# Preparing the second layer's weights half a period after the first layer's, in a two-layer attention kernel on one core

## The chip, the cores and the metric

The kernel runs on one core of a Trainium2 chip. The metric is the device time of one execution in microseconds. Before the change the median of three runs is 3221.76 us (3221.34 to 3221.77).

## What is computed

The input is x of shape [16, 512, 128]. Two blocks follow one another, each of the form x + s * silu(f):

```python
xn = layernorm(x)
s  = gated_conv(xn)          # projection, two causal depthwise convolutions of 32 taps, gates, projection
g  = silu(local_ffn(xn))     # DEPTH = 2 layers, see below
x  = x + s * g
xn = layernorm(x)
s  = attention16(xn)         # 16 heads of 8 with rope
g  = silu(soft_moe(xn))      # 8 experts of 64 slots
x  = x + s * g
```

The part that the change touches is the two-layer function. Each of its layers does

```python
q, k, v = split(shift_token(x) @ wqkv)          # 8 heads of 64
q = rotary(l2norm(q) * qs); k = rotary(l2norm(k) * ks)
x = x + local_attention(q, k, v, window=64) @ wo
h = layernorm(shift_token(x)) * lg + lb
a, gate = split(h @ w1 + b1)                    # 2 x 341 columns
x = x + (a * gelu(gate)) @ w2 + b2
```

## The kernel before

**Streams.** The 16 batches run through stages that are Python generators: L0 (first layer, `layer(b, 0)`), L0b (second layer, `layer(b, 1)`), A (the sum of the first block and the projections of the second, `pre`), S1 and S2 (the attention with 16 heads), M (the experts, `moe`). Two more generators run once: C, the convolution of all batches (`conv`, lines 741 to 853), and P, the preparation of the weights (`setup`, lines 225 to 279).

**Order.** Lines 935 to 954 merge the generators with a heap. PLAN gives each stage a start and a length in periods, a period being the time of one batch; each `yield` returns a weight, and the next piece of a generator is due at its last due time plus weight / total * length. Pieces are written out in the order in which they are due. That order is the priority with which a scheduler then places the instructions on the queues of the engines (TensorE or PE, VectorE or DVE, ScalarE or ACT, GpSimd or POOL, and SP, which issues nearly all DMAs). Each queue runs in order, and an instruction that waits holds up all that stand behind it. C starts at -0.2 of a period and takes 1.8; P starts at -0.01 with a length of 0.009, so nearly the whole of it is due before the first layer's first piece at 0.0. L0b of batch 0 is due from 1.43 on.

**What P does.** It loads small tables (lg, wcol, qkb, line 227 to 234), the rotation tables rt (line 237), and fills `mean` with 1/128 (line 239). Then, for each layer l: six products of rt with the head scales make rot (lines 242 to 251); four pieces of wqkv are loaded (line 254), split into a rounded part and its remainder (lines 256 and 257) and written to the DRAM tensor wqd (line 258); wo, w1 and w2 are loaded (lines 260 to 263); b1 is corrected with six small matmuls (line 268) and sums (line 269); w1 is scaled and freed of its mean (lines 270 to 274), split (lines 276 and 277) and written to the DRAM tensor w1d (line 278).

**What L0 does.** `proj(c)`, for four pairs of heads, loads a piece of wqd on POOL's queue (line 323), multiplies (lines 221 to 223), and forms squares, rotated values and norms on ScalarE, VectorE and POOL (lines 335 to 355). `turn` transposes (lines 364 and 367), `attend` computes the attention (lines 379 to 418). Line 429 loads w1 from w1d, line 433 applies wo, lines 460 to 472 are the second half of the layer.

**What C does.** Its first part goes through the 16 batches: load x into one of two buffers xA (line 771), statistics (lines 146 to 154), scaling (line 776), store of xnd (line 777), transposes (line 780), store of xnTd (line 782), products into Z (lines 789 and 790). L0 of batch b reads xnd and xnTd. Then come the 13 steps of the Toeplitz products (lines 798 to 824) and the 24 output steps (lines 826 to 850), and all of it a second time for the other half of the channels, with the sums read from `part` (line 835) and the result written to s0d (line 844), which stage A reads. After it `late` (line 855) loads the weights of the second block.

**Buffers.** NBUF (lines 30 to 35) gives the number of buffers of each ring of tiles; a tile takes the next buffer of its ring and waits until the last reader of the old tile is done. P draws on the rings of the layers: "q" (4), "wq" (2), "rt" (2), "kT" (2), "w1" (1). The experts' ring "sb" has 2 buffers, for e (lines 679 and 724), ct (line 726) and slT (line 698). All of M's products and transposes take their PSUM bank from "a", which has one buffer and which A, S1 and S2 use as well (lines 36 and 37).

Of the kernel before, what the change touches and what calls it, by code (L numbers as in the profile page):

```python
# [10 lines left out]
F32 = mybir.dt.float32  # L11
F32R = mybir.dt.float32r
AF = mybir.ActivationFunctionType
ALU = mybir.AluOpType
# [8 lines left out]
HID = 341  # L23
CH = [(0, 128), (128, 128), (256, 85)]
# [20 lines left out]
TOT = {"C": 204.0, "P": 11.0, "L0": 93.0, "A": 24.0, "S1": 57.0, "S2": 52.6, "M": 33.0}  # L45
# [48 lines left out]
def bc_row(ap, parts):  # L94
    return ap.rearrange("(o d) -> o d", o=1).to_broadcast([parts, ap.shape[0]])


def body(ctx, tc, a):
    nc = tc.nc
    NB = a["x"].shape[0]  # L100
    V, S, G, PE = nc.vector, nc.scalar, nc.gpsimd, nc.tensor
    dma = nc.sync.dma_start
    bcp = NW * NB

    const = ctx.enter_context(tc.tile_pool(name="const", bufs=1))
# [86 lines left out]
    def mk(sid, b, dflt):  # L192
        def tl(shape, tag, dt=F32):
            cnt[0] += 1
            tg = f"{tag}{sid}"
            return pools[sid].tile(shape, dt, tag=tg, name=f"{tag}{sid}_{b}_{cnt[0]}", bufs=NBUF.get(tg, 2))

        def pt_(nm, tag=dflt):
            cnt[0] += 1
            alt = TAIL.get((tag, NB - b))  # L200
            if alt:
                turns_[tag] = turns_.get(tag, 0) + 1
                tag = alt[turns_[tag] % len(alt)]
            return psb.tile([128, 512], F32, tag=TAGS[tag], name=f"{nm}{sid}_{b}_{cnt[0]}", bufs=NPSUM[TAGS[tag]])

        def quad(src, nm, tag=dflt):
            pt = pt_(nm, tag)
            for p in range(4):
                PE.transpose(pt[:, p * 128 : p * 128 + 128], src(p), ident)  # L209
            return pt  # L210

        def split(pt, tag):
            t = tl([128, 2, 512], tag, F32R)
            S.copy(t[:, 0, :], pt)
            V.tensor_tensor(t[:, 1, :], pt, t[:, 0, :].bitcast(F32), ALU.subtract)  # L215
            return t

        return tl, pt_, quad, split

    def mm3(out, lh, ll, rh, rl, start=True, stop=True):  # L220
        PE.matmul(out, lh, rh, start=start, stop=False)  # L221
        PE.matmul(out, lh, rl, start=False, stop=False)  # L222
        PE.matmul(out, ll, rh, start=False, stop=stop)  # L223

    def setup():
        tl, pt_, quad, split = mk("0", 0, "tr0")
        lg = tl([128, 4], "lg")
        dma(out=lg, in_=a["lgb"])
        dma(out=b1.rearrange("p l k j -> p (l k j)"), in_=a["b1p"])
        wcol = tl([128, 1], "wc")  # L230
        dma(out=wcol, in_=a["wcol"])
        dma(out=maskf.rearrange("p i k -> p (i k)"), in_=a["mask"])
        qkb = tl([128, 2, 2, 64], "q")
        dma(out=qkb.rearrange("p l i d -> p (l i d)"), in_=bc_row(a["qks"], 128))
        V.tensor_scalar(qkb[:, :, 0, :], qkb[:, :, 0, :], 8.0, None, ALU.mult)
        rt = tl([128, 4, 4, 64], "rt")
        dma(out=rt.rearrange("p i n d -> p (i n d)"), in_=a["rot"])
        mean = tl([128, 128], "kT")
        G.memset(mean, 1.0 / 128.0)
        yield 1  # L240
        for l in range(2):
            for i in range(4):
                sc = qkb[:, l, i // 2, :]
                if i % 2:
                    for k in range(2):
                        V.tensor_tensor(
                            rot[:, l, 1, :, i // 2, 32 * k : 32 * k + 32], rt[:, i, :, 32 * k : 32 * k + 32],
                            sc[:, None, 32 - 32 * k : 64 - 32 * k].to_broadcast([128, 4, 32]), ALU.mult,
                        )
                else:  # L250
                    V.tensor_tensor(rot[:, l, 0, :, i // 2, :], rt[:, i], sc[:, None, :].to_broadcast([128, 4, 64]), ALU.mult)
            for c in range(4):
                w = tl([128, 384], "q")
                dma(out=w, in_=a["wqkv"][l, :, 384 * c : 384 * c + 384])
                wt = tl([128, 2, 384], "wq", F32R)
                V.tensor_copy(wt[:, 0, :], w)
                V.tensor_tensor(wt[:, 1, :], w, wt[:, 0, :].bitcast(F32), ALU.subtract)
                dma(out=wqd[l, c].bitcast(F32), in_=wt.bitcast(F32))
                yield 1
            dma(out=wo[:, l], in_=a["wo"][l].rearrange("(c p) d -> p c d", p=128))  # L260
            w1 = tl([128, 2 * HID], "rt")
            dma(out=w1, in_=a["w1"][l])
            dma(out=w2[:, l].rearrange("p j d -> p (j d)"), in_=a["w2p"][l])
            V.tensor_scalar(w2[:, l, 2, :], w2[:, l, 2, :], wcol, None, ALU.mult)
            for k in range(2):
                for j, (r, n) in enumerate(CH):
                    pb = pt_("pb")
                    PE.matmul(pb[:n, 0:1], w1[:, k * HID + r : k * HID + r + n], lg[:, 2 * l + 1 : 2 * l + 2], start=True, stop=True)
                    V.tensor_tensor(b1[:n, l, k, j : j + 1], b1[:n, l, k, j : j + 1], pb[:n, 0:1], ALU.add)
            V.tensor_scalar(w1, w1, lg[:, 2 * l : 2 * l + 1], None, ALU.mult)  # L270
            for k in range(2):
                pb = pt_("pb")
                PE.matmul(pb[:, 0:HID], mean, w1[:, k * HID : k * HID + HID], start=True, stop=True)
                V.tensor_tensor(w1[:, k * HID : k * HID + HID], w1[:, k * HID : k * HID + HID], pb[:, 0:HID], ALU.subtract)
            ws = tl([128, 2, 2 * HID], "w1", F32R)
            V.tensor_copy(ws[:, 0, :], w1)
            V.tensor_tensor(ws[:, 1, :], w1, ws[:, 0, :].bitcast(F32), ALU.subtract)
            dma(out=w1d[l].bitcast(F32), in_=ws.bitcast(F32))
            yield 1

    def load_x(tl, b, tag):
        x = tl([128, 4, 128], tag)
# [572 lines left out]
    def late():  # L855
# [83 lines left out]
        "L0": lambda b: layer(b, 0, box), "L0b": lambda b: layer(b, 1, box), "A": pre, "S1": first, "S2": second,  # L939
        "M": lambda b: moe(b, xrs, prs),  # L940
        "C": lambda b: conv(), "P": lambda b: setup(),
    }
    tot = dict(TOT, L0b=TOT["L0"])
    heap = [(b + st, k, b, nm, ln, make[nm](b)) for b in range(NB) for k, (nm, st, ln) in enumerate(PLAN)]
    heap.append((CONV0, -1, 0, "C", CONV, make["C"](0)))
    heap.append((-0.01, -2, 0, "P", 0.009, make["P"](0)))
    heapq.heapify(heap)
    acc = {}
    while heap:
        t, k, b, nm, ln, gen = heapq.heappop(heap)  # L950
        w = next(gen, None)
# [60 lines left out]
def program(arrays):  # L1012
    import concourse.bacc as bacc

    nc = bacc.Bacc("TRN2", target_bir_lowering=False, num_devices=1)
    a = {}
    named = {}
    for k, v in arrays.items():
        named[f"in_{k}_dram"] = v
        a[k] = nc.dram_tensor(f"in_{k}_dram", v.shape, mybir.dt.from_np(v.dtype), kind="ExternalInput").ap()  # L1020
    a["out"] = nc.dram_tensor("out_0_dram", arrays["x"].shape, F32, kind="ExternalOutput").ap()
    with tile.TileContext(nc, schedule_with_timeline_sim=TLS) as tc, ExitStack() as ctx:
        body(ctx, tc, a)
    return nc, named
# [8 lines left out]
```

## Time and profile before

The page is that of one profiled execution.

| what | value |
|---|---|
| median of three runs | 3221.76 us |
| profiled execution, its own time | 3220.23 us |
| span of the profile | 3218.4 us |
| mean granted clock of TensorE | 0.974 |
| busy: PE | 2932.7 us, 91% of the span |
| busy: PEld, DVE, ACT, POOL | 2173.2, 2334.5, 2071.7, 1596.0 us |
| the chain that ended last | PE 57%, DVE 17%, ACT 13%, POOL 5%, issue 4%, DMA 3% |
| DMA | 251.55 MB, mean 78 GB/s; 249 GB/s in the first of 40 slices |

The span lacks 1.83 us of the execution's own time. A slice is 80.5 us long. "PEld" is the loading of weights into TensorE, "SPq" the issuing of DMAs by SP, "granted clock" the share of full speed that TensorE ran at. A line of a timeline has the start and the length in us, the engine, the line of the kernel, the operation, the tile written and the tile read, how many instructions it stands for, and in brackets the idle time before it and what ended it. An arrow reads "written from".

### The profile page before, as it was taken

Reading aid. Unit: us, or ns where it says so; the run is one execution under the profiler, and the core shown is the slowest. Engines: PE = TensorE matmul, PEld = TensorE weight load, DVE = VectorE, ACT = ScalarE, POOL = GpSimd, SP = SyncE. Lnnn points to the kernel's source line nnn. Section 1 sums busy time; section 2 is a strip of 40 time slices with the busy share of each in tenths; the row PEclk is TensorE's granted clock in tenths of the full one; section 3 lists DMA queues with packets and bytes.
Section 4 is the critical chain, followed back from the end, with each engine's and each line's share of the span. In section 5 each row is a group of like instructions: output and inputs, shape, how many; then the busy total and the mean of one; then the engine's idle time right before and its main releaser. Section 6 shows DMA issues by size and latency. Waiting matters only on the chain.

```text
span 3218.4 us, 67550 instructions
## 1 busy us (share of the span) xinstructions
PE 2932.7 (91%) x24164; PEld 2173.2 (68%) x24164; DVE 2334.5 (73%) x7165; ACT 2071.7 (64%) x4803; POOL 1596.0 (50%) x1854
## 2 busy tenths in 40 slices
PE   5798878889999999999999999999999999999897
PEld 4687756566767767676767677676767676666553
DVE  5779567768777877777787778777777778776563
ACT  2645445657766766676666667676766766656565
POOL 2424366655546473745556464747465564542200
PEclk7999979999999999999999999999999999999998
DMA  7555443122222222222222221221222222211110
GB/s 249 146 141 131 109 118 95 51 81 65 79 65 66 64 79 73 53 82 61 79 66 84 58 76 54 78 73 53 83 59 80 67 82 57 72 51 50 29 46 18
DMA packets 199549, 251.55 MB, mean 78 GB/s; under 512 B 57488, under 2 KB 123184, under 8 KB 199216
## 3 DMA queue, kind: packets, MB, share of 16 engines
q1 hardware_dynamic: 180784, 196.90, 21.4%
q0 software_dynamic: 18432, 50.34, 6.0%
q8 instruction: 193, 3.16, 0.4%
q14 instruction: 140, 1.15, 0.1%
HBM read 159.84 MB, written 57.50 MB: 68 GB/s over the span
## 4 chain that ended last, share of the span: by engine, by line
PE 57%; DVE 17%; ACT 13%; POOL 5%; issue 4%; DMA 3%; SPq 1%; POOLq 0%; DVEq 0%; ACTq 0%
PE pvd L602 7%; PE s2d L618 5%; PE s1c L583 5%; PE pw L433 3%; DVE mw L584 3%; ACT sd L620 3%; PE pw L471 3%; PE sc L379 2%; PE pq L221 2%; PE prT L209 2%; PE ppb L714 2%; DVE pr L392 2%; ACT pr L396 2%; PE pq L223 2%; PE pq L222 2%
## 5 line engine op out<-in xcount | busy, mean ns | idle before, releaser
L584 DVE TENSOR_REDUCE mw<-s1c 128x1 f32<-128x512 f32 x1024 | 697.9, 685 | 260.3 <-PE s1c L583 253.0
L620 ACT ACTIVATE sd<-s2d 128x512 f32<-128x512 f32 x1024 | 612.4, 603 | 331.5 <-PE s2d L618 325.2
L618 PE MATMUL s2d<-QS,KS 128*128 128x512 f32 x1024 | 479.6, 471 | 44.7 <-ACT sd L620 39.7
L583 PE MATMUL s1c<-KS,QS 128*128 128x512 f32 x1024 | 454.5, 446 | 51.8 <-DVE mw L584 43.5
L354 POOL TENSOR_TENSOR y<-ss,mhalf 128x8 f32<-128x8 f32 x256 | 429.6, 1678 | 15.6
L396 ACT ACTIVATE pr<-pr,m 128x128 f32<-128x128 f32 x1024 | 333.6, 396 | 107.9 <-DVE m L392 107.8
L352 POOL TENSOR_SCALAR ss<-ss 128x8 f32<-128x8 f32 x256 | 62.1, 242 | 641.8 <-DVE ss L348 621.7
L618 PEld LDWEIGHTS s2d<-QS,KS 128*128 128x128 f32 x1024 | 192.2, 188 | 237.7 <-issue 114.3
L350 POOL TENSOR_TENSOR rt<-rt,q 128x512 f32<-128x512 f32 x256 | 328.0, 1281 | 3.5 <-DVE q L341 3.5
L335 ACT ACTIVATE q<-pq 128x256 f32<-128x256 f32 x512 | 197.4, 385 | 143.7 <-PE pq L223 136.0
L355 POOL TENSOR_TENSOR rt<-rt,y 128x512 f32<-128x512 f32 x256 | 268.7, 1050 | 16.2
L583 PEld LDWEIGHTS s1c<-KS,QS 128*128 128x128 f32 x1024 | 193.6, 189 | 121.1 <-DVE mw L584 92.4
L337 DVE TENSOR_TENSOR rt<-pq,rot 128x256 f32<-128x256 f32 x512 | 212.4, 415 | 73.1 <-ACT vbuf L336 48.9
L602 PE MATMUL pvd<-sd,Vt 128*32 128x512 f32 x2048 | 249.2, 605 | 1.9 <-ACT sd L620 1.9
L221 PE MATMUL pq<-wq,hT 128*128 128x384 f32 x512 | 207.3, 405 | 25.1 <-DVE q L341 16.9
L341 DVE TENSOR_TENSOR q<-pq,rot 128x256 f32<-128x256 f32 x512 | 212.7, 415 | 0.0
L348 DVE TENSOR_REDUCE ss<-q 128x8 f32<-128x512 f32 x256 | 174.3, 681 | 50.8 <-ACT q L335 50.3
L209 PE MATMUL prT<-step,pr 128*128 128x128 f32 x1024 | 189.6, 281 | 15.3 <-ACT pr L396 10.5
L401 ACT COPY pt<-prT 128x512 f32<-128x512 f32 x256 | 152.3, 595 | 63.8 <-PE prT L209 61.1
L223 PE MATMUL pq<-wq,hT 128*128 128x384 f32 x512 | 178.6, 349 | 1.4 <-DVE hT L215 0.4
L323 POOL DMA_DIRECT2D wq<-wqd x128 | 81.4, 636 | 197.8 <-PE pq L223 140.4
L222 PE MATMUL pq<-wq,hT 128*128 128x384 f32 x512 | 178.8, 349 | 0.0
(255 smaller groups left out, 7435.9 us busy)
## 6 DMA issues: line engine op xcount, KB each, us to landing
wq<-wqd POOLq DMA_DIRECT2D x128, 384.0 KB, 3.7
w<-w1d SPq DMA_DIRECT2D x32, 682.0 KB
vsbuf<-vbuf SPq DMA_DIRECT2D x128, 130.0 KB
QS<-scq SPq DMA_DIRECT2D x128, 128.0 KB
KS<-sck SPq DMA_DIRECT2D x128, 128.0 KB
vsbuf<-vbuf SPq DMA_DIRECT2D x128, 97.5 KB
scq<-sa SPq DMA_DIRECT2D x96, 128.0 KB
sck<-sa SPq DMA_DIRECT2D x96, 128.0 KB
```

Source lines behind the costliest of these rows:

```text
L209: PE.transpose(pt[:, p * 128 : p * 128 + 128], src(p), ident)
L221: PE.matmul(out, lh, rh, start=start, stop=False)
L222: PE.matmul(out, lh, rl, start=False, stop=False)
L350: G.tensor_tensor(rf, rf, t2.rearrange("t p d -> t (p d)"), ALU.add)
L354: G.tensor_tensor(y.rearrange("t p g -> t (p g)"), sh, mhalf[:, 0:8], ALU.pow)
L355: G.tensor_tensor(rt[:, ps], rt[:, ps], y[:, :, :, None].to_broadcast([128, 2, 4, 64]), ALU.mult)
L396: S.activation(pr[:, hh, p, :], pr[:, hh, p, :], AF.Exp, bias=m[:, hh, p : p + 1], scale=-1.0)
L583: PE.matmul(sc, QS[:, g // 2, qt * 128 : qt * 128 + 128], KS[:, g % 2, :], start=True, stop=True)
L584: V.tensor_reduce(mx[:, g, qt : qt + 1], sc, AX.X, ALU.max)
L602: return PE.matmul(pv[32 * q : 32 * q + 32, :], Vt[:, kt, 9 * hd : 9 * hd + 32], e, start=(last == 1 and kt == 1), stop=(last == 3 and kt ...
L618: PE.matmul(sc, KS[:, g % 2, kt * 128 : kt * 128 + 128], QS[:, g // 2, :], start=True, stop=True)
L620: S.activation(e, sc, AF.Exp, scale=ISQ8)
```

## The change

P keeps the first layer. The preparation of a layer becomes a generator of its own, `weights(l)`; P runs `weights(0)`, and `weights(1)` is put on the heap from 0.5 of a period on with a length of 0.3. The four small tables (lg, wcol, qkb, mean) move from the layers' rings into tiles of their own, since both generators read them, and the table rt is loaded once per layer. The ring "sb" goes from 2 buffers to 1. The arithmetic is the same.

```diff
-    "sb": 2, "Db": 1, "gmb": 2, "xrb": 2, "xTb": 1, "prb": 1,
+    "sb": 1, "Db": 1, "gmb": 2, "xrb": 2, "xTb": 1, "prb": 1,
...
+    setup_state = []
+
     def setup():
         tl, pt_, quad, split = mk("0", 0, "tr0")
-        lg = tl([128, 4], "lg")
+        lg = const.tile([128, 4], F32, name="lg")
...
-        wcol = tl([128, 1], "wc")
+        wcol = const.tile([128, 1], F32, name="wcol")
...
-        qkb = tl([128, 2, 2, 64], "q")
+        qkb = const.tile([128, 2, 2, 64], F32, name="qkb")
...
-        rt = tl([128, 4, 4, 64], "rt")
-        dma(out=rt.rearrange("p i n d -> p (i n d)"), in_=a["rot"])
-        mean = tl([128, 128], "kT")
+        mean = const.tile([128, 128], F32, name="mean")
         G.memset(mean, 1.0 / 128.0)
         yield 1
-        for l in range(2):
-            for i in range(4):
...
+        setup_state.append((lg, wcol, qkb, mean))
+        yield from weights(0)
+
+    def weights(l):
+        lg, wcol, qkb, mean = setup_state[0]
+        tl, pt_, quad, split = mk("0", 0, f"tr{l}")
+        rt = tl([128, 4, 4, 64], "rt")
+        dma(out=rt.rearrange("p i n d -> p (i n d)"), in_=a["rot"])
+        for i in range(4):
...
-    tot = dict(TOT, L0b=TOT["L0"])
+    tot = dict(TOT, L0b=TOT["L0"], P1=5.0)
...
     heap.append((-0.01, -2, 0, "P", 0.009, make["P"](0)))
+    heap.append((0.5, -3, 0, "P1", 0.3, weights(1)))
```

The body of `weights` is that of the old loop over l, with the same lines in the same order. Its small matmuls take their PSUM bank from the tag "tr0" for the first layer and from "tr1" for the second, where both took "tr0" before. In the changed file the lines from `setup` on are 7 or 8 higher.

More of the change, by code (lines that the diff above doesn't have):

```diff
@@ L234, in setup @@
         dma(out=qkb.rearrange("p l i d -> p (l i d)"), in_=bc_row(a["qks"], 128))
         V.tensor_scalar(qkb[:, :, 0, :], qkb[:, :, 0, :], 8.0, None, ALU.mult)
+        mean = const.tile([128, 128], F32, name="mean")
+        G.memset(mean, 1.0 / 128.0)
+        yield 1
+        setup_state.append((lg, wcol, qkb, mean))
[3 more added lines that the diff above has]
+        tl, pt_, quad, split = mk("0", 0, f"tr{l}")
         rt = tl([128, 4, 4, 64], "rt")
@@ L237, in setup @@
         dma(out=rt.rearrange("p i n d -> p (i n d)"), in_=a["rot"])
-        mean = tl([128, 128], "kT")
-        G.memset(mean, 1.0 / 128.0)
-        yield 1
-        for l in range(2):
-            for i in range(4):
[L243 to L279, printed above, removed]
@@ new lines, in weights @@
+        for i in range(4):
+            sc = qkb[:, l, i // 2, :]
+            if i % 2:
+                for k in range(2):
+                    V.tensor_tensor(
+                        rot[:, l, 1, :, i // 2, 32 * k : 32 * k + 32], rt[:, i, :, 32 * k : 32 * k + 32],
+                        sc[:, None, 32 - 32 * k : 64 - 32 * k].to_broadcast([128, 4, 32]), ALU.mult,
+                    )
+            else:
+                V.tensor_tensor(rot[:, l, 0, :, i // 2, :], rt[:, i], sc[:, None, :].to_broadcast([128, 4, 64]), ALU.mult)
@@ new lines, in weights @@
+        for c in range(4):
+            w = tl([128, 384], "q")
+            dma(out=w, in_=a["wqkv"][l, :, 384 * c : 384 * c + 384])
+            wt = tl([128, 2, 384], "wq", F32R)
+            V.tensor_copy(wt[:, 0, :], w)
+            V.tensor_tensor(wt[:, 1, :], w, wt[:, 0, :].bitcast(F32), ALU.subtract)
+            dma(out=wqd[l, c].bitcast(F32), in_=wt.bitcast(F32))
+            yield 1
+        dma(out=wo[:, l], in_=a["wo"][l].rearrange("(c p) d -> p c d", p=128))
+        w1 = tl([128, 2 * HID], "rt")
@@ new lines, in weights @@
+        dma(out=w1, in_=a["w1"][l])
+        dma(out=w2[:, l].rearrange("p j d -> p (j d)"), in_=a["w2p"][l])
+        V.tensor_scalar(w2[:, l, 2, :], w2[:, l, 2, :], wcol, None, ALU.mult)
+        for k in range(2):
+            for j, (r, n) in enumerate(CH):
+                pb = pt_("pb")
+                PE.matmul(pb[:n, 0:1], w1[:, k * HID + r : k * HID + r + n], lg[:, 2 * l + 1 : 2 * l + 2], start=True, stop=True)
+                V.tensor_tensor(b1[:n, l, k, j : j + 1], b1[:n, l, k, j : j + 1], pb[:n, 0:1], ALU.add)
@@ new lines, in weights @@
+        V.tensor_scalar(w1, w1, lg[:, 2 * l : 2 * l + 1], None, ALU.mult)
+        for k in range(2):
+            pb = pt_("pb")
+            PE.matmul(pb[:, 0:HID], mean, w1[:, k * HID : k * HID + HID], start=True, stop=True)
+            V.tensor_tensor(w1[:, k * HID : k * HID + HID], w1[:, k * HID : k * HID + HID], pb[:, 0:HID], ALU.subtract)
+        ws = tl([128, 2, 2 * HID], "w1", F32R)
+        V.tensor_copy(ws[:, 0, :], w1)
+        V.tensor_tensor(ws[:, 1, :], w1, ws[:, 0, :].bitcast(F32), ALU.subtract)
@@ L281, in load_x @@
+        dma(out=w1d[l].bitcast(F32), in_=ws.bitcast(F32))
+        yield 1
     def load_x(tl, b, tag):
```

## The prediction

> **What bounds the kernel now.** I read four views: the 40 slices, the chain that ended last, a table of stages over the first 500 us, and the timelines of single queues in the first 70 us. First the slices of the whole span.
>
> ```profile
> PE   5798878889999999999999999999999999999897
> ...
> DVE  5779567768777877777787778777777778776563
> ...
> PEclk7999979999999999999999999999999999999998
> DMA  7555443122222222222222221221222222211110
> ```
>
> TensorE is at nine tenths from the tenth slice (724 us) to the end, and its total is 91% of the span. DMA is the busiest resource only in the first slice. So from there the time is a stream of TensorE work in a fixed order, and a change of the opening counts by how much earlier that stream starts. The scheduled orders of the two kernels bear this out: from TensorE row 1380 (the projections of the first A stage, near 478 us) on, the two lists are the same row for row, but for some ten rows near the end that stand a little earlier or later. What the first 480 us gain or lose is handed on almost unchanged.
>
> The opening by stages (columns: window, busy us of PE, PEld, DVE, ACT, POOL with instruction counts, granted clock, DMA share, GB/s):
>
> ```profile
> 0.00:50.00 50.00, 23.03 (x96) 17.61 (x96) 30.74 (x114) 10.76 (x22) 7.28 (x28) 0.80 0.89 286
> 50.00:100.00 50.00, 34.03 (x219) 27.45 (x220) 27.29 (x112) 23.64 (x65) 27.85 (x33) 0.75 0.56 170
> 100.00:150.00 50.00, 40.10 (x374) 34.06 (x375) 36.29 (x126) 29.10 (x74) 26.51 (x30) 0.90 0.50 146
> 150.00:200.00 50.00, 44.54 (x428) 41.74 (x427) 39.15 (x93) 25.28 (x51) 3.95 (x6) 0.97 0.50 128
> ```
>
> And, in the same columns, cut at other places:
>
> ```profile
> 140.00:180.00 40.00, 32.42 (x383) 30.10 (x384) 34.49 (x87) 20.16 (x41) 0.04 (x1) 1.00 0.64 162
> 180.00:260.00 80.00, 76.92 (x703) 72.66 (x702) 59.59 (x135) 35.89 (x87) 28.60 (x31) 0.98 0.48 136
> 15.00:60.00 45.00, 30.16 (x130) 23.55 (x131) 30.22 (x103) 14.09 (x34) 6.74 (x11) 0.70 0.97 323
> ```
>
> From 15 to 60 us the DMA engines are full (0.97, 323 GB/s) and TensorE is not. TensorE is idle for 53 us of the first 150. From 140 to 180 us VectorE is the fullest (86%, the Toeplitz loop), from 180 to 260 us TensorE (96%).
>
> Now the queues.
>
> ```profile
> 41.33 0.43 SPq L771 DMA_DIRECT2D xA<-in_x_dram  x1
> 45.07 0.39 SPq L771 DMA_DIRECT2D xA<-in_x_dram  x1
> ...
> 60.59 1.66 SPq L771 DMA_DIRECT2D xA<-in_x_dram  x2
> ```
> ```profile
> 49.97 0.78 POOL L323 DMA_DIRECT2D wq<-wqd  x1 [0.31 <-issue]
> ```
> ```profile
> 52.61 1.63 PE L780 MATMUL ptA<-step,xA 128*128 128x128 f32 x4 [7.80 <-ACT xA L776]
> 54.20 0.69 PE L221 MATMUL pq<-wq,hT 128*128 128x384 f32 x1
> ```
>
> The convolution's batches 4 and 5 are loaded at 41 and 45 us, 6 and 7 at 60.6. The first projection of the attention layer starts at 54.2 us although its input is ready at 46: its weight load is issued at 49.97, because the ring of two "wq" buffers passes through the four splits of layer 1 first (the last write to wqd is issued at 47.45), and it stands on POOL's queue behind batch 4's statistics (49.42).
>
> **The change, part by part.**
>
> *Layer 1's weights leave the start.* Removed from the full DMA window: four reads of 192 KB and four writes of 384, w1 341 and its write 682, wo 256, w2 192: 3775 KB, and batch 0's own read of w1 (682 KB, issued at 52.4) moves behind it too. At 323 GB/s that is 12.0 + 2.2 = 14 us of DMA time, not all of it on a path. Followed through the new order: batch 2's load is issued as before (20.97) and lands about when it did; its store goes out near 32 instead of 33.35 and now lands in some 3.5 us, so batch 4 is loaded at 35.6 instead of 41.33 and lands in 3.9 instead of 6.8 (3.0 to 4.0 are the landings of later loads in the chain of waits). Its statistics start at 39.5 instead of 48.1. But in the new order projection 0's VectorE and POOL rows now stand ahead of batch 4's scaling; with their durations (POOL 1.28, 1.67 and 1.04, VectorE 8 x 0.41 and a reduction of 0.7) batch 5 is scaled by 52.2 instead of 56.4, and batch 6 is loaded at 54 instead of 60.6: **convolution 6.5 us earlier**. The first projection starts when wqd's third write of layer 0 has landed, about 34.5: **attention stream 20 us earlier**, and it fills the 7.80 us hole above.
>
> *The same work comes back at half a period.* In the order it stands beside batches 12 to 15 of the convolution and the first Toeplitz steps, 115 to 150 us of before. VectorE rows for one layer: 4 x 0.36 + 4 x 0.56 (split), 4 x 0.29 + 2 x 0.42 (rot), 6 x 0.15, 0.29, 0.57, 2 x 0.51, 0.51, 0.86 = 9.8 us; TensorE 6 small products and 2 x 0.74. Some 3.9 us of VectorE (bias sums, scaling, mean, w1 split) fall in the Toeplitz loop, where VectorE is on the path: cost 3.9. The other 5.9 lie where VectorE is 69% busy: 0 to 2. Taken: +3.5, bounds 0 and +6. The table of rotations is read a second time (512 KB, 1.6 us at 323 GB/s) with DMA at 0.44: nothing, or 1.6 if that cover is gone.
>
> *New waits.* Layer 1's pieces take turns in the rings "rt" (2), "wq" (2), "q" (4) and "w1" (1) with the running layer. The second rotation load waits on SP for the transposes of projection 2; behind it on SP stand the store of batch 14, the write-back of its transposed copy and the next w1 load. In TensorE's order these transposes come before batch 14's, so I take 0. Below 0 it can't be; above, it is six round trips (four splits, rotations, w1) of a load and a store of 3.4 us each, 6.8 a trip and 41 in all, of which the attention stream has its lead over the convolution in hand, 20 - 6.5 = 13.5.
>
> *TensorE's order.* Summing matmul rows by their durations, 5.0 us more of the attention layer stands ahead of the first L830 transpose, and 2.8 us more ahead of the convolution's last product. In the TensorE-bound stretch from 180 us more work done is time gained: at equal work the lead is -6.5 + 3.5 - 5.0 = -8.0. The convolution's end, which lets the A stage begin, leads by 8.0 - 2.8 = 5.2. What follows needs both: between -5.2 and -8.0. **Taken: -7.**
>
> *Small tables in places of their own, "sb" from 2 to 1.* Four loads land in other tiles: nothing. The ring "sb" holds e, ct and slT of the expert stage, and with one buffer each has to be read before the next is written. The waits before its rows:
>
> ```profile
>   DVE mb L723: 18.6, 26
>   DVE ri L414: 16.8, 11
>   ACT sb L680: 8.0, 17
> ```
>
> ScalarE waits there for the maximum of the next product, and that product has one PSUM bank ("a", one buffer), which the copy or the sum after the last reader of e frees. The bank already forces the turn; cost 0. If it did not, each of 16 batches would lose up to 4 x 0.6 us (an L727 copy), 38 in all. The Trainium skill ("Trainium Kernel Development and Optimization", Best Practices) advises double buffers so that transfers and work overlap; by it this edit would cost. No transfer uses this ring, so the rows decide and the sum stays.
>
> On the clock: the window after the 7.80 us hole was granted 0.50. "TensorE: Matmul & The Clock Gate" (What's actually happening) says that an idle window of about 3.4 us halves the clock. By it the filled hole gives back half of the 7.3 us of matmuls between 50 and 60 us; TensorE isn't the limit there, so the sum stays either way.
>
> **Sum.** The profiled execution took 3220.23 us, span 3218.4 with 1.83 around it: 3220.23 - 7 = 3213.2. The median of the three runs stands 1.53 above the profiled one: **3214.8**.
>
> **Rivals.**
> 1. *The lead is absorbed* (0.22). The convolution's second output loop is a chain of its own (read of part 2.4, sum 0.7, six s0d issues of 0.33), and the A stage waits for SP's loads until 460 us. For it: TensorE is only 75 to 83% busy from 360 to 420. Against: that chain starts earlier too. Gain 0 to 3: 3220.5.
> 2. *The whole 20 us lead of the attention stream counts* (0.15): if TensorE, not the convolution, bounds everything from 180 us. Against: granted clock 0.50 and 12 of 20 us busy at 440 to 460, a wait for the convolution's end. Gain 12 to 16: 3207.5.
> 3. *Slower* (0.13): the ring turns above. SP stands still when a layer-1 load waits for a buffer that a late attention step holds, with the convolution's loads behind it. For it: SP serves both streams in one order, and DMA carries 0.44 to 0.64 there. Against: in the new order these buffers' last readers stand ahead. It decides from three stopped trips (20.4 us = 13.5 in hand and 7 gained) on; four give 27.2 - 20.5 = +6.7: 3228.5.
> 4. *The one buffer of "sb" bites* (0.03): up to +38 in the steady part, less the 7: 3250.
>
> The forecast has 0.47 and spans -4 to -11 (3211 to 3218).
>
> **Numbers.** A measurement of this kernel can tell some 0.2% (6.4 us, below 3215.3) from no change. Faster: 0.27 of the forecast's 0.47 plus rival 2's 0.15, in all 0.42. Within: 0.20 plus rival 1's 0.22, in all 0.42. Slower: rivals 3 and 4, 0.16. The range from 3206 to 3225 takes in the forecast, rival 1, most of 2 and the mild end of 3.
>
> **What would show it.** The first L221-type product near 35 us; batch 4's load near 36; DMA share from 60 us back near its old level and higher between 115 and 150; the first output transposes of the convolution near 175 (before: 179.2); the first product of the A stage 5 to 8 us earlier; the distance from there to the end unchanged within 1 us. A POOL or SP wait above 5 us between 100 and 150 us would speak for rival 3; a growing distance in the steady part, for rival 4.

## The result, and the profile after

The changed kernel takes **3232.48 us** in the median (3224.01 to 3238.3); the kernel before, run beside it, 3225.93 (3221.34 to 3231.77). The ratio is **1.0029** with an interval of 1.0016 to 1.0042: the change costs 9.3 us (5.2 to 13.5), where 7 were to be gained. A second series (run e16_again) gives 1.0028 (1.0016 to 1.0040). Ratios below are always to the kernel before, run beside the kernel in question; 0.001 is 3.22 us.

The profiled execution is the slowest of its eight: 3238.3 us, span 3236.5. Its lines are 7 or 8 higher than in the kernel before. First the slices of the page:

```profile
PE   5798878889999999999999999999999999999897
...
PEclk8899979999999999999999999999999999999998
DMA  6555443122212222122222222222222222211110
```

At this grain next to nothing is seen: in the first slice DMA is lower (6 for 7) and the clock higher (8 for 7), in the second the clock is lower (8 for 9). The stages tell more (columns as above: us busy of PE, PEld, DVE, ACT, POOL, clock, DMA share, GB/s):

```profile
0.00:50.00 50.00, 21.02 (x89) 14.86 (x89) 26.15 (x99) 12.18 (x28) 11.96 (x34) 0.83 0.80 245
50.00:100.00 50.00, 35.77 (x273) 28.34 (x274) 30.74 (x129) 29.86 (x82) 32.92 (x38) 0.84 0.42 132
100.00:150.00 50.00, 37.13 (x333) 31.51 (x331) 35.91 (x116) 21.99 (x52) 17.18 (x19) 0.81 0.60 193
150.00:200.00 50.00, 41.37 (x364) 36.45 (x363) 39.12 (x95) 22.66 (x46) 5.96 (x8) 0.97 0.61 160
```

From 50 to 100 us TensorE does more than before, at a better clock (35.77 us at 0.84 for 34.03 at 0.75). From 100 to 200 it does less (37.13 at 0.81 for 40.10 at 0.90, then 41.37 for 44.54), while DMA stands at 0.60 for 0.50. The gain was there and was lost again just where the second layer's work has been put.

The single queues that the prediction named, SP, POOL and TensorE in turn:

```profile
41.16 0.38 SPq L778 DMA_DIRECT2D xA<-in_x_dram  x1
45.55 0.38 SPq L778 DMA_DIRECT2D xA<-in_x_dram  x1
```
```profile
33.28 0.78 POOL L330 DMA_DIRECT2D wq<-wqd  x1 [0.64 <-DMA wqd<-wq]
```
```profile
40.81 0.42 PE L221 MATMUL pq<-wq,hT 128*128 128x384 f32 x1
```

The attention stream starts 13.4 us earlier (40.81 for 54.20), not 20: the load of wq goes out in time (33.28), but 7.5 us pass until its first use. Batch 4 of the convolution is loaded no earlier in this profile (41.16 for 41.33; 38.5 in the second profile of the same kernel, e16_again), batch 6 at 58.5 for 60.6. Two of the second layer's loads have not left the start: wo and w2, which no ring holds back, are issued at 25.00 and 26.05 us.

A quantity that helps from here on: busy time of TensorE times granted clock, roughly the work done in us of full clock (roughly, since the clock is a mean over idle time too). Five kernels in one window (100 to 140 us), in order: before, after, e3_none, e9_transfers, e13_few_bytes, each from its own table of windows:

```profile
100.00:140.00 40.00, 32.34 (x273) 26.77 (x273) 27.74 (x110) 24.46 (x66) 26.47 (x30) 0.87 0.44 136
```
```profile
100.00:140.00 40.00, 28.18 (x224) 23.55 (x222) 27.74 (x102) 17.33 (x44) 17.02 (x19) 0.77 0.63 209
```
```profile
100.00:140.00 40.00, 29.94 (x308) 25.58 (x308) 27.54 (x98) 23.13 (x59) 14.57 (x16) 0.96 0.51 151
```
```profile
100.00:140.00 40.00, 27.79 (x244) 23.16 (x243) 22.84 (x83) 16.99 (x43) 16.35 (x19) 0.83 0.57 182
```
```profile
100.00:140.00 40.00, 31.81 (x292) 25.07 (x292) 24.07 (x100) 23.16 (x60) 16.34 (x19) 0.88 0.49 147
```

Worked out for all four stages (busy times clock, from the same tables), with the milestones of the opening and the time beside it:

| kernel | 0-60 | 60-100 | 100-140 | 140-200 | first Toeplitz product | first output transpose | A's first product | ratio |
|---|---|---|---|---|---|---|---|---|
| before | 23.3 | 21.1 | 28.1 | 50.7 | 135.8 | 179.2 | 478.2 | 1 |
| after | 22.9 | 25.1 | 21.7 | 48.8 | 140.2 | 191.3 | 483.8 | 1.0029 |
| e16_again | 23.8 | 23.6 | 21.4 | 48.3 | 141.8 | 192.6 | 486.7 | 1.0028 |
| e3_none | 25.2 | 28.1 | 28.7 | 54.5 | 126.0 | 171.1 | 467.9 | 0.9981 |
| e10_rows | 32.0 | 28.6 | 28.9 | 50.9 | 128.3 | 174.9 | 472.1 | 0.9990 |
| e9_transfers | 28.2 | 27.7 | 23.1 | 50.8 | 135.5 | 180.5 | 485.4 | 1.0010 |
| e13_few_bytes | 23.8 | 23.6 | 28.0 | 49.8 | 137.8 | 189.3 | 482.4 | 0.9988 |
| e11_both | 32.2 | 25.0 | 27.4 | 50.5 | 138.4 | 188.6 | 478.9 | 1.0018 |

Two profiles with one and the same order of TensorE's opening (before and e1_sb1) have A's first product at 478.2 and 473.2 us, and e2_start, with a somewhat other order and the same work at the start, at 479.8: a single profile's opening is good to some 3 us. The profiled executions also lie at different places among their kernel's runs: that of e3_none is its fastest (3208.6 us; median 3215.9), that of after its slowest. After's two profiles lose 6.5 us of work from 100 to 140 us and 2 more up to 200, against before.

What happens there is in the chain of waits of the kernel after (start, length in us, what):

```profile
115.89 4.31 DMA xA<-in_x_dram
...
126.86 3.01 DMA rt<-in_w_dram
129.92 0.59 PE pb L275 x2
130.51 0.96 PE prT L209 x4
131.47 0.22 PE pb L275 x2
131.68 0.53 PE ptA L787 x2
...
135.98 1.50 PE pz L796 x6
137.50 0.81 DVE Z L797
138.37 1.81 POOL Z L804
140.22 1.95 PE pc L816 x20
```

Read it downwards. The convolution's last batch (xA) is loaded at 115.89 and lands at 120.2, in a stretch in which the DMA engines are full (share 1.01 from 118 to 120 us, 1.03 from 120 to 122): the second layer's table, its third and fourth pieces of wqkv and a write of wqd are issued between 116.4 and 119.7. Even so this load took 4.31 us, against 3.72 in the kernel before. Then 6.6 us on VectorE: the batch's statistics, a norm, four maxima, the rotations (3.5 us, 123.4 to 126.8). Then the load of the second layer's w1, issued at 126.86, 5.9 us after SP's last issue had ended: it needs a buffer of the ring rt. TensorE's bias product L275 waits for that load, and behind it in TensorE's queue stand the attention's transposes (prT), the transposes of the last batch (ptA) and its products (pz), after which the Toeplitz steps can begin. From 120 to 130 us TensorE was busy for 2.37 us, and from 126 to 130 its clock was granted at 0.50, from 130 to 140 at 0.54. (The Trainium skill, "TensorE: Matmul & The Clock Gate", What's actually happening, has an idle window halve the clock; these rows agree.)

The stretch from the issue of that load to the first Toeplitz product shows where the time goes. First the last batch in before (its statistics start, its scaling starts), then the same two rows of after with a pair of the rotation rows between them:

```profile
124.56 0.87 DVE L146 BATCH_NORM_STATS2 stA<-xA 128x6 f32<-128x128 f32 x4 [0.58 <-DMA xA<-in_x_dram]
128.19 1.65 ACT L776 ACTIVATE xA<-xA,mr,rsA 128x128 f32<-128x128 f32 x4 [0.54 <-DVE mr L774]
```
```profile
120.22 0.87 DVE L146 BATCH_NORM_STATS2 stA<-xA 128x6 f32<-128x128 f32 x4 [1.90 <-DMA xA<-in_x_dram]
123.70 1.55 DVE L253 TENSOR_TENSOR rot<-rt,qkb 128x128 f32<-128x128 f32 x2
130.11 1.65 ACT L783 ACTIVATE xA<-xA,mr,rsA 128x128 f32<-128x128 f32 x4 [0.58 <-DVE mr L781]
```

| kernel | load to landing | landing to scaling | scaling to first Toeplitz product | sum |
|---|---|---|---|---|
| before | 3.7 | 3.7 | 7.6 | 15.0 |
| after | 4.3 | 9.9 | 10.1 | 24.3 |
| e16_again | 4.2 | 9.9 | 10.2 | 24.3 |
| e3_none | 3.8 | 5.7 | 9.3 | 18.8 |
| e13_few_bytes | 4.7 | 9.1 | 6.4 | 20.2 |

After issues the load 4.9 us earlier than before and has its first Toeplitz product 4.4 us later. Of the 9.3 us lost between, 0.6 are the landing and 6.2 stand between landing and scaling. There VectorE's queue holds the second layer's rotations (3.5 us) and three split rows (some 1.2 us). A pair of rotation rows takes 0.49 us at the start of before; here the two pairs took 1.55 and 1.33, and why isn't shown. But e13_few_bytes, which has no second-layer rows there, takes nearly as long (9.1 us), so these rows are not shown to be what costs. And part of after's lag to e3_none is older than all this: batch 12 is loaded at 97.5 (98.9 in e16_again, 90.9 in e3_none), ahead of the second layer's first load of wqkv at 106.1. That part stays unexplained.

### The profile page after: what moved, and what is told of

Read it like the earlier page. It is cut to its first block, busy times and chain, and to the rows that moved or that the text cites. A ratio compares the mean times of both kernels' runs of the same rounds, so it can differ in the third digit from the quotient of the medians.

```text
span 3236.5 us, 67563 instructions
## 1 busy us (share of the span) xinstructions
PE 2947.3 (91%) x24164; PEld 2181.7 (67%) x24164; DVE 2337.6 (72%) x7165; ACT 2069.0 (64%) x4803; POOL 1596.5 (49%) x1854
## 4 chain that ended last, share of the span: by engine, by line
PE 58%; DVE 16%; ACT 13%; POOL 5%; DMA 4%; issue 4%; SPq 1%; POOLq 0%; DVEq 0%; ACTq 0%
PE pvd L609 6%; PE s2d L625 6%; PE s1c L590 5%; PE pw L440 3%; DVE mw L591 3%; PE pw L478 3%; ACT sd L627 3%; PE sc L386 3%; PE prT L209 2%; PE pq L221 2%; DVE pr L399 2%; PE ppb L721 2%; PE pq L223 2%; PE pq L222 2%; ACT pr L403 2%
## 5 line engine op out<-in xcount | busy, mean ns | idle before, releaser
L342 ACT ACTIVATE q<-pq 128x256 f32<-128x256 f32 x512 | 196.7, 384 | 128.7 <-PE pq L223 127.9
L221 PE MATMUL pq<-wq,hT 128*128 128x384 f32 x512 | 207.3, 405 | 32.1 <-DVE q L348 21.1
L209 PE MATMUL prT<-step,pr 128*128 128x128 f32 x1024 | 193.7, 285 | 22.9 <-ACT pr L403 18.6
## 6 DMA issues: line engine op xcount, KB each, us to landing
vsbuf<-vbuf SPq DMA_DIRECT2D x128, 97.5 KB
```

## Experiments

**e1_sb1**: the ring alone.

```diff
-    "sb": 2, "Db": 1, "gmb": 2,
+    "sb": 1, "Db": 1, "gmb": 2,
```

> The kernel before with the one edit of the ring sb from 2 buffers to 1. The medians are 3225.9 us before and 3232.5 after, and in the profiles the first product of stage A stands at 478.2 us before and 483.8 after. Theory 1 (the opening is later because the second layer's VectorE work stands in front of the convolution's last batches) and theory 2 (it is later because the attention stream that runs ahead takes the engines from the convolution) both give the time before, within 0.1%, and no growth of lag from 480 us to the end beyond what the granted clock makes. Theory 3 (the single buffer costs in the steady part, from where the profile after has 8 us more of its lag between 600 and 1160 us) gives 5 to 10 us more than before.

3220.32 us, ratio 0.9992 (0.9981 to 1.0004). The single buffer costs nothing; theory 3 falls. In after's own trace the wait before these rows is that of before to the tenth:

```profile
  DVE mb L730: 18.6, 26
```

**e2_start**: everything but the delay.

```diff
-    heap.append((0.5, -3, 0, "P1", 0.3, weights(1)))
+    heap.append((-0.001, -3, 0, "P1", 0.0005, weights(1)))
```

> The kernel after, but the second layer's weights are due right behind the first layer's, so that its order is that of before; the tables stay in places of their own, the rotation table is read twice, sb has 1 buffer. Theories 1 and 2 give the time before within 0.1% (A's first product 476 to 481 us), since the delay alone is what costs. Theory 3, or a cost of the second table read or of the new places, gives 5 us more than before.

3219.29 us, 0.9993 (0.9983 to 1.0003), A's first product at 479.8. New places and a second load of the table cost nothing that the interval shows. The effect is in the delay. (TensorE's order isn't quite that of before, against the expectation, but the second layer's work does stand at the start.)

**e3_none**: the second layer's preparation is gone.

```diff
-    heap.append((0.5, -3, 0, "P1", 0.3, weights(1)))
...
-            G.dma_start(out=wq, in_=wqd[l, c])
+            G.dma_start(out=wq, in_=wqd[0, c])
```

and so for rot, w1d, wo, b1 and w2.

> The kernel after without the second layer's preparation: its layer works with the first layer's weights, rotations and biases, so the output is another. The start is as free as in the kernel after, and nothing comes back at half a period. Theory 1 gives the lead that was forecast: 8 to 14 us faster than before, 3212 to 3218 us, A's first product at 464 to 470 us, and the convolution's output transposes begin at 170 to 175 us. Theory 2 gives within 4 us of the kernel after, A's first product at 479 to 484 us, output transposes from 185 us on.

3215.88 us, 0.9981 (0.9972 to 0.9989): 6.1 us faster. Output transposes begin at 171.1, A's first product at 467.9. The lead that the prediction saw in the opening is real, and theory 2 falls. Between 0.9981 and after's 1.0029 lie **15.5 us (some 5 either way): that is what the second layer's work costs at 0.5 of a period**, its loads of wo and w2, which stay at the start, included.

**e4_engines**: VectorE relieved.

```diff
+        E, C = (V.tensor_tensor, V.tensor_copy) if l == 0 else (G.tensor_tensor, S.copy)
...
-            V.tensor_copy(wt[:, 0, :], w)
-            V.tensor_tensor(wt[:, 1, :], w, wt[:, 0, :].bitcast(F32), ALU.subtract)
+            C(wt[:, 0, :], w)
+            E(wt[:, 1, :], w, wt[:, 0, :].bitcast(F32), ALU.subtract)
```

and so for the rotations and the split of w1.

> The kernel after with the second layer's rotation products and splits taken from VectorE: rounding copies on ScalarE, products and remainders on POOL; 7.5 of some 10 us of VectorE work leave its queue. Theory 1 gives 5 to 10 us less than after (3222 to 3228 us; A's first product 473 to 479 us), unless POOL, which also forms the batches' statistics, takes the same place. Theory 2 gives after's time within 3 us.

3236.8 us, 1.0044 (1.0031 to 1.0057): no better. The timeline of its POOL shows why the expectation's "unless" came true:

```profile
122.10 0.88 POOL L254 TENSOR_TENSOR rot<-rt,qkb 128x128 f32<-128x128 f32 x2
123.06 0.23 POOL L152 TENSOR_SCALAR veA<-mvA 128x4 f32<-128x4 f32 x1
```

The variance of the last batch (veA; its input was ready at 119.3) stands behind the rotations, which now are POOL's (119.91 to 122.98). The rows hold the same batch in another queue. The first Toeplitz product does come earlier than in after (135.5 for 140.2), but the output transposes don't (191.8 for 191.3). This run doesn't tell theories 1 and 2 apart.

**e5 to e8**: the same work at 0.2, 0.8, 0.95 and 1.1 of a period.

```diff
-    heap.append((0.5, -3, 0, "P1", 0.3, weights(1)))
+    heap.append((0.2, -3, 0, "P1", 0.3, weights(1)))
```

> The kernel after with the second layer's weights from 0.2 of a period on instead of 0.5: its pieces stand among the convolution's batches 8 to 14. Without them the median is 6 us below before (run e3_none), with them at 0.5 it is 9 above (3232.5 against some 3223), so they cost some 15 us there. Theory 1 (it is the place: in-order queues of VectorE, POOL and SP, between the last batches of the convolution and in the Toeplitz loop) gives a cost between none and 15 that depends on the place; here each piece still stands in front of a batch's statistics, but none in the Toeplitz loop: 3219 to 3228 us, the first Toeplitz product at 132 to 138 us and output transposes at 176 to 182. Theory 4 (the work costs its 15 us wherever it is put behind the start, by its transfers and its ring turns) gives 3228 to 3234 us.

> The second layer's weights from 0.8 of a period on: nearly all behind the first Toeplitz loop, in the stretch from 175 us on where TensorE is the fullest and VectorE has room. Theory 1 gives back most of the lead: the first Toeplitz product at 125 to 128 us, output transposes at 170 to 174, A's first product at 468 to 474, a median of 3216 to 3221 us. Theory 4 gives 3228 to 3234 us.

> The second layer's weights from 0.95 of a period on, in the output steps and later. Theory 1: as from 0.8 on, 3215 to 3221 us, A's first product at 468 to 474 us. Theory 4: 3228 to 3234 us. A loss that comes only here, with the second layer's first projection late, would be a third thing: the weights are then due too near to their use.

> The second layer's weights from 1.1 of a period on, which ends at 1.4, just before the second layer's first piece at 1.43. Theory 1: 3215 to 3221 us if the writes are done in time; each split, write and read back takes some 7 us in turn, and if they stand in the way of the second layer's first projections, up to 14 us more than the run from 0.8 on. Theory 4: 3228 to 3234 us.

| start | ratio | first Toeplitz product | first output transpose | A's first product |
|---|---|---|---|---|
| 0.2 | 1.0082 (1.0066 to 1.0099) | 147.1 | 197.8 | 495.5 |
| 0.5 (after) | 1.0029 (1.0016 to 1.0042) | 140.2 | 191.3 | 483.8 |
| 0.8 | 1.0006 (0.9996 to 1.0017) | 126.6 | 171.2 | 481.3 |
| 0.95 | 0.9999 (0.9988 to 1.0011) | 124.0 | 168.7 | 478.1 |
| 1.1 | 1.0016 (1.0005 to 1.0027) | 124.7 | 169.3 | 477.9 |

The place decides: theory 4 falls. But the later places gain nothing either, against the expectation. Up to the output transposes the lead is 8 to 10.5 us; then it is given back. In e7_p095 TensorE's work from 200 to 330 us is 105.8 us (busy 110.23, clock 0.96) where before has 116.0 (117.21, 0.99) and e3_none 114.1. At 0.2 two things add up: 17 us are lost up to A's first product, and the steady part is slower, which the last section tells. What becomes of the lead between 200 and 330 us isn't shown row by row.

**e9, e10, e11**: the work taken apart, each added to e3_none and due at 0.5.

```diff
+            wt = tl([128, 2, 384], "wq", F32R)
+            for h in range(2):
+                dma(out=wt[:, h, :].bitcast(F32), in_=a["wqkv"][l, :, 384 * c : 384 * c + 384])
+            dma(out=wqd[l, c].bitcast(F32), in_=wt.bitcast(F32))
```

is a piece of e9_transfers; in e10_rows the same piece is

```diff
+            V.tensor_copy(dst[:, 0:384].bitcast(F32R), src[:, 0:384])
+            V.tensor_tensor(dst[:, 384:768].bitcast(F32R), src[:, 0:384], dst[:, 0:384], ALU.subtract)
```

on parts of rot, and e11_both has both.

> Run e3_none (nothing of the second layer is prepared, 6 us below before) plus, at 0.5 of a period, only the second layer's transfers: its reads land in buffers of the rings rt, wq and w1 and are written on to the DRAM tensors, with SP's waits and the ring turns, but nothing is computed on them; the second layer works with the first one's weights, so the output is another. 15 us lie between e3_none and after. Theory 5 (SP's stops and ring turns hold the convolution's loads and the first layer's wq loads): most of the 15 us are here, 3225 to 3233 us, the first Toeplitz product from 135 us on. Theory 6 (VectorE's and TensorE's rows in front of the last batches): within 4 us of e3_none, 3216 to 3220 us, the first Toeplitz product at 126 to 130 us.

> Run e3_none plus, at 0.5 of a period, only the second layer's computing: the same rows on VectorE and TensorE in shape and number, on tiles that are long there, with nothing loaded, nothing stored, no ring turn and no wait for a landing; the output is another. Theory 6: most of the 15 us are here, 3225 to 3233 us, the first Toeplitz product from 135 us on. Theory 5: only their bare time where VectorE is the limit, 3 to 4 us above e3_none, 3218 to 3222 us, the first Toeplitz product at 127 to 131 us. Theory 7 (it is the coupling: rows that stand in a queue and wait for a landing or for a store) gives both runs, this and e9_transfers, within 5 us of e3_none.

> Run e3_none plus the transfers of e9_transfers and the rows of e10_rows, side by side at 0.5 of a period and independent of each other: no row waits for a landing and no store for a row; the output is another. Theory 7 (coupling) gives 3218 to 3224 us, clearly below the kernel after; theories 5 and 6 give after's time, 3229 to 3235 us, since the parts add up without the coupling.

| run | median | ratio | above e3_none | last batch scaled at |
|---|---|---|---|---|
| e3_none | 3215.88 | 0.9981 (0.9972 to 0.9989) | 0 | 116.7 |
| e10_rows | 3220.84 | 0.9990 (0.9980 to 1.0000) | 2.9 us | 119.8 |
| e9_transfers | 3225.77 | 1.0010 (0.9997 to 1.0024) | 9.3 us | 127.9 |
| e11_both | 3227.76 | 1.0018 (1.0007 to 1.0029) | 11.9 us | 130.9 |
| after | 3232.48 | 1.0029 (1.0016 to 1.0042) | 15.5 us | 130.1 |

(Each difference of two ratios has some 4 to 5.5 us of uncertainty.) The table can't be read as the work's parts at their place, since much of the work doesn't stand there. In e10_rows the added rows wait for nothing, and the scheduler put all of them at the start, between 16.6 and 36.4 us; of TensorE's and VectorE's:

```profile
16.91 0.42 DVE L302 TENSOR_TENSOR rot<-rot,qkb 128x256 f32<-128x256 f32 x1
29.65 0.78 PE L316 MATMUL pb<-rot,mean 128*128 128x341 f32 x1
35.59 0.85 DVE L319 TENSOR_TENSOR rot<-rot 128x682 fp32r<-128x682 f32 x1
```

So the 2.9 us are the price of the rows in the opening. In e11_both they stand there too. What the rows cost in front of the last batches, theory 6, was not measured by any run. In e9_transfers the pieces of wqkv and the table do stand at 88 to 114 us, but wo and w2 are issued at 24 to 26 and w1 from 38 us on, and each piece of wqkv and w1 is read twice, once for each half of its buffer (1109 KB more than the second layer's real transfers). Its 9.3 us (4 to 14) show that transfers of this kind cost without a row; how much of it is the real transfers' price in after, the run doesn't show. Theory 7 (all coupling) would put both runs within 5 us of e3_none; e10_rows says nothing on it, and e9_transfers lies above, but not by more than the uncertainty. In e9_transfers VectorE stands for 5.92 us, waiting for the last batch:

```profile
124.26 0.87 DVE L146 BATCH_NORM_STATS2 stA<-xA 128x6 f32<-128x128 f32 x4 [5.92 <-DMA xA<-in_x_dram]
```

Its load was issued at 114.77: 9.5 us to land, where e3_none's (issued at 107.2) took 3.8. The kernel after has no such landing (4.3 us, 4.2 in e16_again).

**e12_split**: half of the work at the start, half at 0.95.

```diff
         yield from weights(0)
+        yield from weights(1, rest=False)
...
+    heap.append((0.95, -3, 0, "P1", 0.3, weights(1, first=False)))
```

> A version meant to beat both kernels: the second layer's rotations and its wqkv are prepared at the start as in the kernel before, and only its w1, w2, wo and the bias (half of the bytes, 4 of 10 us of VectorE) from 0.95 of a period on, where the run e7_p095 lost nothing against before. If half of the opening's lead of 6 to 10 us is kept and the part that comes back costs half of the 6 us that e7_p095 lies above e3_none: 3219 to 3223 us, 0 to 4 below before. If the opening is bound by something that the first half holds as well, the time before, 3222 to 3225 us.

3226.92 us, 1.0015 (1.0005 to 1.0026). It beats neither e7_p095 nor before.

**e13_few_bytes** and **e18_bytes**: stops or bytes?

```diff
-                dma(out=wt[:, h, :].bitcast(F32), in_=a["wqkv"][l, :, 384 * c : 384 * c + 384])
+                dma(out=wt[0:16, h, :].bitcast(F32), in_=a["wqkv"][l, 0:16, 384 * c : 384 * c + 384])
```

(e13, and so for each transfer); in e18 the copies go from DRAM to DRAM:

```diff
+            dma(out=xq[c], in_=src)
+            for h in range(2):
+                dma(out=wqd[l, c, :, h, :].bitcast(F32), in_=src)
```

> Run e9_transfers with every transfer of the second layer cut to 16 of its 128 partitions: the same instructions on SP, the same waits and ring turns, an eighth of the bytes; the output is another. Theory 5a (the bytes: from 114 to 122 us the DMA engines are full, and the last batch of the convolution lands late): back to e3_none, within 3 us of 6 below before, 3214 to 3219 us; the last batch is scaled by 120 us (128 in e9_transfers) and the first Toeplitz product starts at 126 to 130. Theory 5b (SP's stops and the ring turns): as e9_transfers, 3223 to 3228 us, first Toeplitz product from 133 us on.

> The counterpart of e13_few_bytes: run e3_none plus the bytes of the second layer's transfers as copies from DRAM to DRAM, issued on SP at 0.5 of a period like the others, but with no buffer of a ring and so with no wait of SP and no ring turn; the output is another. 5a (bytes): near e9_transfers, 0 to 5 us above before, and TensorE again does little between 100 and 140 us (busy times clock about 23 us, as in e9_transfers, where e13_few_bytes has 28). 5b (stops): near e3_none, 4 to 8 us below before.

e13: 3220.9 us, 0.9988 (0.9977 to 0.9998). With an eighth of the bytes and all of the stops, 7.1 of the 9.3 us are gone (1.6 to 12.6): a little above the 3219 us that 5a allows, below 5b's 3223. TensorE's work from 100 to 140 us is 28.0 us again (e9_transfers: 23.1). But the place expected for it was wrong: the last batch is scaled at 131.3, later than in e9, and TensorE is simply not idle meanwhile, as attention work is there to do. So how late the last batch is isn't by itself what costs. Nor does the rest of the opening show the gain: up to 100 us TensorE did less than in e9 (47.4 for 55.9 us of work), the first output transpose comes 8.8 us later (189.3 for 180.5) and A's first product 3.0 us earlier (482.4 for 485.4). The two profiled executions lie 12.1 us apart, and some 9 of these arise behind A's first product, where nothing of the second layer's preparation is left. That the bytes are the greater part is thus not shown; the medians alone speak for it.

e18: 3229.14 us, 1.0020 (1.0010 to 1.0030), but it doesn't answer its question. With nothing to wait for, the copies were placed at 24 to 46 us, and the opening was full again (DMA share 0.87 up to 60 us, e3_none 0.76; work of TensorE 19.2 us for 25.2). It does show that transfers alone, without rows or ring turns, can eat the lead of the opening: put there, these copies cost 12.6 us (8 to 17) against e3_none.

**e14_rot05, e15_rot095, e17_rotlate**: the rotations elsewhere. In e14 and e15 both layers' are made at the start from one load, in e17 the second layer's at 0.95:

```diff
+        for m in range(2 if l == 0 else 0):
...
+    heap.append((0.5, -3, 0, "P1", 0.3, weights(1, rots=False)))
+    heap.append((0.95, -4, 0, "P2", 0.1, weights(1, rest=False)))
```

> The kernel after, but the rotations of both layers are made at the start from one load of the table, as in the kernel before; the rest of the second layer's weights stays at 0.5 of a period. It takes 512 KB out of the full stretch from 114 to 122 us and 3.3 us of VectorE from in front of the maxima. If these bytes are what delays the last batch (5a): 4 to 8 us below after, 3224 to 3229 us. If it is the turns of q, wq and w1 with their stops (5b): within 2 us of after.

> A version meant to beat both: the rotations of both layers at the start from one load, the rest of the second layer's weights from 0.95 of a period on. e7_p095 equals before; without the second table load and 3 us of VectorE beside the output steps it should gain 1 to 4 us, and lose up to 1 at the start for 3.3 us of VectorE there: 3218 to 3223 us, against 3222 before.

> The kernel after with the second layer's rotations (512 KB of table and 3.3 us of VectorE) moved on to 0.95 of a period, while the splits and the rest stay at 0.5. It is e14_rot05 without a change at the start, and TensorE's order from 700 us on is the common one, which e14_rot05 had lost. If the bytes in the full stretch are what costs (5a): a quarter of some 7 us for bytes and the rows' share, 2 to 5 us below after, 3227 to 3230 us against 3223 before. If the stops do it (5b): within 2 us of after, 3230 to 3234 us.

e14: 3244.56 us, 1.0069 (1.0056 to 1.0082); e15: 3234.9, 1.0035 (1.0022 to 1.0049); e17: 3231.72, 1.0029 (1.0018 to 1.0040). None helps. e14 is spoilt by another order of its whole steady part (last section). In e15 the first layer's third and fourth splits come 4 us later (first projection at 44.5 us, 40.8 in e7_p095), and the first Toeplitz product at 135.4 where e7_p095 has 124.0: 4 us at the start have become 11. In e17 the chain runs through the splits, which now stand where the rotations stood, and again through the bias products: last batch scaled at 130.8, as in after. Taking the table's 512 KB out of the full stretch is thus not enough, against 5a's numbers.

**e16_again**: the kernel after once more.

> The kernel after once more, timed beside the three others: 8 to 11 us above before (ratio 1.0025 to 1.0035), A's first product at 481 to 487 us, the last batch of the convolution scaled at 127 to 132 us and the first Toeplitz product at 134 to 142. From that product to the end its profile should be no longer than that of before but for low-clock windows: if theory 3 (a cost in the steady part) had anything to it, the distance from A's first product to the end, 2752.7 us in the profile after and 2740.2 before, would be above 2748 again.

3230.31 us, 1.0028 (1.0016 to 1.0040); last batch scaled at 131.6, first Toeplitz product at 141.8, A's first product at 486.7, and from there 2742.1 us to the end of the span, where before has 2740.2 and the profile after 2752.7. Of the 7 us that the first profile lost between 600 and 1160 us the second lost 4 and later won them back: they are not seen to be a cost of the change.

## Why the prediction was wrong, point by point

The forecast of 7 us gained is made of some 10.5 us gained at the start less 3.5 for the work that comes back. Measured are 6.1 us gained (e3_none, 3.5 to 9) less 15.5.

- *Layer 1's weights leave the start.* Right in kind, and measured without the rest by e3_none: output transposes 8.1 us earlier (171.1 for 179.2), A's first product 10.3 in its fastest execution, the median time 6.1. The terms in it were off: batch 4 is loaded at 41.2 (38.5 in e16_again), not 35.6, as batch 2's store goes out at 35.28, not near 32, and the attention stream leads by 13.4, not 20. Of the 3775 KB counted as removed, wo and w2 (448 KB) stayed at the start.
- ***The same work comes back at half a period: +3.5, bounds 0 and +6.* This is the step that failed, with the next one.** It costs 15.5 (10.5 to 20.5). Even by its own parts, 3.9 and 0 to 2, the term was 3.9 to 5.9. The rotations, put at 2.0 us of VectorE, took 3.5 in after and stood between the last batch and its scaling. The transfers were put at "nothing, or 1.6", since DMA stood at 0.44 there; e9_transfers, which moves more bytes than the real ones, lies 9.3 above e3_none without a row. A mean share says nothing of single microseconds: in after DMA stood at 1.01 to 1.03 from 118 to 122 us, though the load that fell into them took only 0.6 us longer than before's.
- *New waits: 0.* Wrong: behind the stop of SP before w1's load, TensorE's bias product waits for that load with the last batch in its back, and the chain from the last batch's load to the first Toeplitz product is 24.3 us long for 15.0. What these waits are worth in the time, no run separates: e13_few_bytes lies 2.2 us above e3_none, less than the uncertainty, but its w1 is loaded at the start.
- *TensorE's order: -5.0; first output transposes near 175.* Not seen in after (191.3), seen in e3_none (171.1): it needed the lead that the returning work ate.
- *Small tables: 0, "sb": 0.* Right (e2_start 0.9993, e1_sb1 0.9992).
- *The distance from the A stage to the end unchanged within 1 us.* In order yes (TensorE's lists agree but for a few rows), in time no: 2740.2, 2752.7, 2742.1. The tolerance was too narrow for one execution.
- *Rivals.* Rival 3 (slower, by ring turns) has the direction, and its signs came: a POOL wait of 5.1 us, an SP stop of 6 and a TensorE wait of 6.6 between 100 and 150 us. But e3_none, which is faster, has an SP pause of 9.2 us there (107.6 to 116.7), so that sign proves little; the one stop seen for a ring turn is not the four that its price counts, and that its +6.7 lies near the measured +9.3 (5.2 to 13.5) is luck as far as is known. Rivals 1, 2 and 4 fall with e3_none, the milestones and e1_sb1. (The granted clock of 0.50 that was held against rival 2 is that of 450 to 460 us; from 440 to 450 it is 0.67.)

What stays open: how the 15.5 us divide between rows, bytes, stops and the wait on w1, since the rows never stood at their place alone; why the convolution lags already at 97 us; and why the places from 0.8 on give back their lead between 200 and 330 us. That the delay costs, and that its place decides how much, is shown; the mechanism is argued from one chain. No kernel here beats the one before; e3_none, which leaves the work out, puts what could be had by this move at 6 us (3.5 to 9).

## What to carry to other kernels

Work that is moved out of a full opening isn't free where an engine's or a queue's mean share is half: look at the few microseconds in which it will meet what a whole stage waits for, in 2 us windows, and at what stands behind each of its instructions in every in-order queue, a small bias product on TensorE included. Price the bytes, the rows and the waits again at the new place, and try three or four places: here the same work, against before, cost from 0 to 26 us, and none of them gained. When the work is taken apart in an experiment, see in the trace that the parts stand where they are meant to: rows and copies that wait for nothing were put at 17 to 46 us here, not at 100.

## What the runs showed that was not expected

*A change of the opening can change the order of everything after.* In e5_p02 and e14_rot05 TensorE's list differs from before's all the way: from A's first product on, with like products in a row counted once, some 3600 rows are added or missing in a list of some 10000, where after has 7. The other runs lie between (e9_transfers 38, e3_none 157, e13_few_bytes 185, e10_rows 610, these mostly up to 1.1 ms), which is one more reason not to read differences of a few us between them as the price of a part. The steady part of e5_p02 and e14_rot05 takes 177.3 and 178.4 us for a batch (ten batches of A's first copy, 1011.28 to 2784.39 and 1005.09 to 2788.84), before 176.2, after 176.4: 11 to 22 us over ten batches, from a piece that was done by 200 us.

*The clock falls at other places in another execution.* After's lag to before grows in jumps of 1 to 2 us, near 685, 770, 920 and 1030 us of before, and the first two are in e16_again too. At each the granted clock is lower than in before's profile for a few microseconds, with the same instructions in the same order. About the same stretch of work in before and in after:

```profile
680.00:685.00 5.00, 4.57 (x59) 3.92 (x60) 4.64 (x18) 3.05 (x5) 2.08 (x2) 1.00 0.59 181
```
```profile
686.60:691.60 5.00, 3.47 (x37) 2.54 (x38) 3.79 (x7) 3.44 (x5) 0.95 (x1) 0.72 0.57 145
```

59 products at 1.00 there, 37 at 0.72 here. What makes the clock fall in one execution and not in the other wasn't found. Medians of one kernel's runs in different series differ by up to 4 us (before: 3221.7 to 3225.9), so only ratios to runs beside it were used.
